# A causal attention stage whose row maxima are placed by batch instead of by group, and whose second score pass follows the first by eight units instead of twelve

## The chip, the core and the metric

The kernel runs on one core of a Trainium2 chip. The metric is the device time of one execution in microseconds, as the median of several runs. A profiled execution gives the trace: every instruction of the engines PE (matmul), PEld (its weight loads), DVE, ACT, POOL, and the DMAs, with start, length, line of the kernel, and what each waited for.

## The reference, cut to what matters

Two adaptive-layernorm transformer layers over 32 sequences of 256 tokens of 128 channels, all in float32. Layer 0 is plain attention and a feed-forward net with 4-bit rounding. Layer 1 is causal attention with 16 heads of 8 channels, then a mixture of experts of which 4 are active and each token takes 2. The change lies in layer 1's attention:

```python
qkv_heads = qkv.reshape(b, heads, s, -1)
q, k, v = jnp.split(qkv_heads, 3, axis=-1)
scale = 1.0 / np.sqrt(2.0 * hidden)
qk = jnp.einsum('bhse,bhte->bhst', q, k) * scale
mask = jnp.triu(jnp.full((s, s), -jnp.inf, dtype=jnp.float32), k=1)
attn = jax.nn.softmax(qk + mask, axis=-1)
out = jnp.einsum('bhst,bhte->bhse', attn, v).reshape(b, s, e)
```

A softmax needs each row's maximum. The kernel finds it in a first pass over the scores and subtracts it in a second.

## The kernel before, in words

The 8192 tokens are 16 groups (`NG`) of 512 (`TPG` = 4 tiles of 128); a group is two sequences, called batches here (`NB2` = 2, index j). The kernel has three stages, one after the other in time: layer 0, whose order is a written-out list of steps; the causal stage, with layer 1's attention and the choice of experts; and the expert stage, which works through tiles of tokens (`load`, `turn`, `tile_of`), and whose first loads need the memory of the causal stage.

The causal stage (from L655 on) is a loop over units, eight per group (`NU` = 8): four per batch, as j = n // 4. Its pieces:

- `maxima(u)` (L866, L873, L877): PE computes the scores c_s of a unit from qx and k and adds the mask; DVE reduces them in two instructions to negative maxima in c_mx.
- `gather_maxima`, `spread_maxima`, `place_maxima` (L887 to L907): once a group, DVE combines the eight units' maxima into c_m (four small instructions), PE transposes it into c_pm (PSUM), DVE copies it to c_mT, and SP writes it with 8 DMAs into a spare column of c_q. That column meets a column of ones in k, so that the second pass yields scores with the maximum already taken off.
- `probs(u)` (L920, L928, L931): PE computes these scores c_t from kx and q, ACT takes exp into c_p in two instructions, POOL zeroes what the mask forbids (two selects).
- `values(u, p)` (L948, L955): PE multiplies by v into c_po; after a batch's last unit DVE transposes c_po into c_o.
- For the next group: `c_start` (DVE statistics, then small POOL instructions), `c_norm` (ACT, xnc), `c_turn` (PE transposes c_xt, ACT makes c_hT), `c_qkv` (PE c_pq, DVE adds the bias into tok), `c_rows` (DVE transposes to q, k, v), `c_apart_q`, `c_apart_v` (ACT), `c_apart_k` (POOL, 1.6 us), `c_v` (PE transposes c_pv, ACT copies to c_vT).
- For groups behind: `c_ratio`, `c_gate` (DVE, and DMAs of the gate rows), `c_add` (POOL), then the d pieces: `d_start`, `d_norm`, `d_keep`, `d_turn` (PE d_xt, ACT d_hT), `d_logits` (PE d_pl, two ACT copies), and once per three groups `d_probs`, `d_share`, `d_rank`, `d_choose`, `d_pair`, `d_count`, `d_place`, and `d_scatter` (POOL indirect DMAs). `tables` (L1196 on, some 23 small DVE instructions) works out from the counts which rows the expert tiles load.

What sets the order is the list `beside` with `put(n, k, lead, piece)`: piece runs at every unit whose position in its group is n, for the group `lead` away; k = 0 is before the unit's `probs`, k = 1 after it. PE, DVE, ACT and POOL run this stage in exactly the written order; SP's DMAs keep close to it. In one step n the order is: `maxima` of unit n, `values` of the unit whose probs came two steps before (`BEHIND` = 2), pieces with k = 0, `probs` of unit n - `LAG`, pieces with k = 1. `LAG` is 12. So for 12 steps there are maxima alone, for 116 steps both, for 12 probs alone, and two more steps for values. What the last groups leave over (`remaining`) is fed into the first tiles of the expert stage.

All PE results of these pieces but c_s, c_t and c_po go through one PSUM buffer: pool `r_ps`, tag `ps`, one buffer. Whoever writes it waits until the one before has been read out. In the positions 1, 3, 5 and 7 of a group it is used by c_v, in 0, 2, 4 and 6 by c_qkv, each with k = 1; by c_turn at 0, spread_maxima at 1, d_turn at 2, d_count at 3, d_logits at 4 and 6, each with k = 0.

Of the kernel before, what the change touches and what calls it, by code (L numbers as in the profile page):

```python
# [10 lines left out]
F32 = mybir.dt.float32  # L11
# [8 lines left out]
P = 128  # L20
# [14 lines left out]
def adaln_two_layers(ctx: ExitStack, tc: tile.TileContext, ins, out: bass.AP):  # L35
    nc = tc.nc
    X = ins["L0_attn_X"].flatten_outer_dims()
    NTOK = X.shape[0]
    NG = NTOK // GT
# [87 lines left out]
    ident = const.tile([P, P], F32, tag="ident", name="ident")  # L127
# [6 lines left out]
    for l in range(2):  # L134
        sc = mp.tile([NB, D], F32, tag=f"sc{l}", name=f"sc{l}")
        nc.scalar.activation(sc, c_sb[l], AF.Silu)
        pt = mps.tile([P, 512], F32, tag="mps", name=f"mps_t{l}")
# [3 lines left out]
        pm = mps.tile([P, 512], F32, tag="mps", name=f"mps_m{l}")  # L141
# [8 lines left out]
        m = const.tile([D, 6, NB], F32, tag=f"mod{l}", name=f"mod{l}")  # L150
# [81 lines left out]
    with ExitStack() as ph:  # L232
# [10 lines left out]
        sb2 = ph.enter_context(tc.tile_pool(name="ab_sb2", bufs=2))  # L243
        sb3 = ph.enter_context(tc.tile_pool(name="ab_sb3", bufs=3))
        sb4 = ph.enter_context(tc.tile_pool(name="ab_sb4", bufs=4))
        ps = ph.enter_context(tc.tile_pool(name="ab_ps", bufs=3, space=PSUM))
# [408 lines left out]
    with ExitStack() as ph:  # L655
        one = ph.enter_context(tc.tile_pool(name="c_one", bufs=1))
        sb2 = ph.enter_context(tc.tile_pool(name="c_sb2", bufs=2))
# [3 lines left out]
        ps = r_ps  # L661
# [49 lines left out]
        NQ = NPOS // B  # L711
        NB2 = TPG // 2
        NU = NB2 * 2 * 2
        NBK = NB2 * 2 * NQ

        SEEN = [[(3, 0, 4 * B), (0, 4 * B, B)], [(2, 0, 3 * B), (1, 3 * B, 2 * B)]]
        SEES = [[(0, B, 4 * B), (3, 0, B)], [(1, 0, 3 * B), (2, 3 * B, 2 * B)]]
# [162 lines left out]
                    AX.X, ALU.max, negate=True,  # L880
                )

        def gather_maxima(g):
            mx = outs.pop(("mx", g)).rearrange("p (u s) l b -> p s u l b", s=2)
            m = sb2.tile([P, 4, NU // 2, NQ], F32, tag="m", name=f"c_m{g}")
            to = lambda b: m.rearrange("p l u b -> p b u l")[:, b, :, :]
            nc.vector.tensor_reduce(to(3), mx[:, 0, :, :, 0:4], AX.X, ALU.min)  # L887
            nc.vector.tensor_copy(to(0), mx[:, 0, :, :, 4])
            nc.vector.tensor_reduce(to(2), mx[:, 1, :, :, 0:3], AX.X, ALU.min)
            nc.vector.tensor_tensor(to(1), mx[:, 1, :, :, 3], mx[:, 1, :, :, 4], ALU.min)  # L890
            outs["m", g] = m

        def spread_maxima(g):

            m = outs.pop(("m", g))
            pt = outs["pm", g] = ps.tile([P, 512], F32, tag="ps", name=f"c_pm{g}")
            nc.tensor.transpose(pt[: 4 * NBK, :P], m.rearrange("p l u b -> p (l u b)"), ident)

        def place_maxima(g):
            pt = outs.pop(("pm", g))  # L900
            q = made[g]["q"].rearrange("p j (b n) -> p (j b) n", n=B)
            mT = sb2.tile([4 * NBK, P], F32, tag="mT", name=f"c_mT{g}")
            nc.vector.tensor_copy(mT, pt[: 4 * NBK, :P])
            for lane in range(4):
                for h in range(2):
                    row = lane * L + h * HR + C
                    nc.sync.dma_start(  # L907
                        q[row : row + 1, :, :], mT[lane * NBK : (lane + 1) * NBK, h * B : (h + 1) * B]
                    )

        def probs(u):
# [284 lines left out]
        def tables(kind):  # L1196
            nt, width = KINDS[kind]
            t = lambda n, shape, ty=F32: (one if kind else dw).tile([1] + shape, ty, tag=f"t_{n}{kind}", name=f"t_{n}{kind}")
            full, whole = t("full", [NP]), t("whole", [NP], I32)
            nc.vector.scalar_tensor_tensor(  # L1200
                full, nxt[0:1, :], float(width - 1) if kind == 2 else 0.0, region, ALU.add, ALU.subtract
            )
            nc.vector.tensor_copy(whole, full)
            nc.vector.tensor_scalar(whole, whole, width.bit_length() - 1, None, ALU.arith_shift_right)
            nc.vector.tensor_copy(full, whole)
            if kind > 0:
                nc.vector.scalar_tensor_tensor(full, done, float(-(ST // width)), full, ALU.mult, ALU.add)
            tri, begin = t("tri", [NP, NP]), t("begin", [NP])
            nc.vector.tensor_tensor(tri, earlier, full.unsqueeze(1).to_broadcast([1, NP, NP]), ALU.mult)
            nc.vector.tensor_reduce(begin, tri, AX.X, ALU.add)  # L1210

            off, last = t("off", [NP]), t("last", [NP])
            nc.vector.scalar_tensor_tensor(off, begin, float(-width), region, ALU.mult, ALU.add)
            if kind > 0:
                nc.vector.scalar_tensor_tensor(off, done, float(ST), off, ALU.mult, ALU.add)
            nc.vector.scalar_tensor_tensor(last, nxt[0:1, :], float(-width), region, ALU.add, ALU.max)
            nc.vector.tensor_tensor(coef[:, 0, :], off[:, 1:], off[:, : NP - 1], ALU.subtract)
            nc.vector.tensor_tensor(coef[:, 3, :], last[:, 1:], last[:, : NP - 1], ALU.subtract)
            past, part, to = t("past", [nt, NP - 1]), t("part", [nt, 4, NP - 1]), t("to", [nt, 4])
            nc.vector.tensor_tensor(  # L1220
                past, number[:, :nt].unsqueeze(2).to_broadcast([1, nt, NP - 1]),
                begin[:, 1:].unsqueeze(1).to_broadcast([1, nt, NP - 1]), ALU.is_ge,
            )
            nc.vector.tensor_tensor(
                part, past.unsqueeze(2).to_broadcast([1, nt, 4, NP - 1]),
                coef.unsqueeze(1).to_broadcast([1, nt, 4, NP - 1]), ALU.mult,
            )
            nc.vector.tensor_reduce(to, part, AX.X, ALU.add)
            nc.vector.tensor_scalar(to[:, :, 0], to[:, :, 0], off[:, 0:1], None, ALU.add)
            nc.vector.scalar_tensor_tensor(to[:, :, 0], number[:, :nt], float(width), to[:, :, 0], ALU.mult, ALU.add)  # L1230
            nc.vector.tensor_scalar(to[:, :, 3], to[:, :, 3], last[:, 0:1], None, ALU.add)
            nc.vector.tensor_tensor(to[:, :, 0], to[:, :, 0], to[:, :, 3], ALU.min)
            nc.vector.tensor_scalar(to[:, :, 2], to[:, :, 2], 1.0, None, ALU.add)
            told[kind] = t("told", [nt, 4], I32)
            nc.vector.tensor_copy(told[kind], to)
            if kind < 2:

                more = t("more", [NP])
                nc.vector.tensor_scalar(more, begin, -1.0, float(nt), ALU.mult, ALU.add)
                nc.vector.tensor_scalar(more, more, 0.0, None, ALU.max)  # L1240
                nc.vector.tensor_tensor(more, more, full, ALU.min)
                nc.vector.tensor_tensor(done, done, more, ALU.add)


        LAG = NU + 4
        BEHIND = 2
        beside = [[[], []] for _ in range(NU)]

        def put(n, k, lead, piece, *more):
            beside[n][k].append((lead, piece, more))  # L1250

        put(1, 0, -1, spread_maxima)
        put(1, 0, -1, place_maxima)
        put(0, 0, 1, c_turn)
        for i in range(TPG):
            put((2 + 2 * i) % NU, 1, 1 - (2 + 2 * i) // NU, c_qkv, i)
        for j in range(NB2):
            for n, k, piece, more in (
# [2 lines left out]
            ):  # L1261
                n += 4 * j
                put(n % NU, k, 1 - n // NU, piece, j, *more)
        put(0, 0, -1, gather_maxima)
        put(6, 0, -2, c_ratio)
        put(7, 0, -2, c_gate)
        put(7, 1, -2, c_add)
        for h in range(2):
            put(4 + 4 * h if h == 0 else 0, 0, 3 - h, c_start, h)
            put(1 + 2 * h, 1, 2, c_norm, h)  # L1270
            put(2 + h, 0, -3, d_start, h)
            put(5 + 2 * h, 1, -3, d_norm, h)
        put(4, 1, -3, d_keep)
        put(2, 0, -4, d_turn)
        put(4, 0, -4, d_logits, 0)
        put(6, 0, -4, d_logits, 1)
        last_of = lambda piece: lambda g, *more: piece(g, *more) if g == batch_of[g][-1] else False
        for n, k, lead, piece, *more in (
            (7, 1, -4, d_probs), (0, 1, -5, d_share), (3, 1, -5, d_rank), (4, 1, -5, d_choose), (5, 1, -5, d_pair, 0),
            (0, 1, -6, d_pair, 1), (1, 1, -6, d_pair, 2), (3, 0, -6, d_count), (4, 1, -6, d_place),  # L1280
        ):
            put(n, k, lead, last_of(piece), *more)
        for k in range(NT):
            put((5 + k) % NU, 1, -6 - (5 + k) // NU, last_of(d_scatter), k)
        put(4, 1, -8, lambda g: tables(0) if g == EARLY else False)
        for kind in (1, 2):
            put(3, 1, -6, lambda g, kind: tables(kind) if g == NG - 1 else False, kind)
        assert max(EARLY * NU + 8 * NU + 4, EARLY * NU + 6 * NU + 5 + NT - 1) < NG * NU + LAG + BEHIND

        def pieces(n, k):  # L1290
            for lead, piece, more in beside[n % NU][k]:
# [22 lines left out]

        def remaining():

            for n in range(len(units) + LAG + BEHIND, (NG + 8) * NU + 4):
                for k in range(2):
                    for lead, piece, more in beside[n % NU][k]:
                        g = n // NU + lead  # L1320
                        if 0 <= g < NG and piece(g, *more) is not False:
                            yield
# [185 lines left out]
```

## Time and profile before

| what | us |
|---|---|
| three runs | 1515.89, 1517.38, 1525.77 |
| median | 1517.38 |
| the profiled execution, its own time | 1526.12 |
| its span, first to last instruction | 1524.4 |
| causal stage in it: first c_s to last c_po | 415 to 962 |
| PE busy, 500 to 550 / 700 to 750 | 47.6 / 47.0 of 50 |
| DVE busy, the same | 41.6 / 42.8 of 50 |
| PE busy, 400 to 450 / 950 to 1000 | 35.0 / 32.4 of 50 |
| granted PE clock, the same | 0.80 / 0.73 |

The page gives busy time by engine, the span in 40 slices (digits are tenths; PEclk is the clock that the throttle granted), the chain that ended last, and groups of instructions. The timeline lists instructions in order of time, with the idle time of the engine before each and what ended it. The windows give busy time by engine for chosen stretches. Busy time of the whole span mixes three stages; the change touches the middle one.

### The profile page before, as it was taken

What the parts mean: (1) busy time and instruction counts of PE and PEld (TensorE: products, weight loads), DVE (VectorE), ACT (ScalarE), POOL (GpSimd) and SP (SyncE); (2) the same over time, 40 slices, a digit from 0 to 9 for tenths busy, and PEclk for the clock granted to TensorE, in tenths of its full rate; (3) what the DMA queues carried; (4) which work ended last, traced back from release to release, by engine and by line L of the source; (5) the groups of instructions that cost most, each with busy time, mean ns of one, the idle gap of its engine ahead of it and who ended that gap; (6) DMA issues with size and microseconds to landing.
All of it is one profiled execution on the core that took longest, in us unless ns stands there. A gap on an engine that the chain in (4) does not pass through costs nothing.

```text
span 1524.4 us, 33395 instructions
## 1 busy us (share of the span) xinstructions
PE 1382.3 (91%) x12505; PEld 1086.6 (71%) x12505; DVE 1001.1 (66%) x2219; ACT 777.8 (51%) x1551; POOL 744.8 (49%) x1079
## 2 busy tenths in 40 slices
PE   5888998987689999999999999598999999999997
PEld 4666665654357766667666667487999999999996
DVE  6799998989487888888988877146333333333332
ACT  5998877843255777767676667141222222222221
POOL 4767866664334665558668567426222222222122
PEclk9999999999799999999999999699999999999999
DMA  8000000000100000002102011856667777777760
GB/s 225 1 1 1 1 1 1 1 1 1 12 2 3 17 14 16 18 6 66 30 24 69 14 44 55 269 171 211 194 184 224 228 217 230 227 212 237 229 188 11
DMA packets 132065, 139.26 MB, mean 91 GB/s; under 512 B 14376, under 2 KB 105968, under 8 KB 131904
## 3 DMA queue, kind: packets, MB, share of 16 engines
q1 hardware_dynamic: 125600, 119.92, 26.9%
q0 software_dynamic: 6304, 17.21, 3.1%
q8 instruction: 99, 1.62, 0.4%
q14 instruction: 62, 0.51, 0.1%
HBM read 116.95 MB, written 19.61 MB: 90 GB/s over the span
## 4 chain that ended last, share of the span: by engine, by line
PE 69%; DVE 19%; ACT 4%; issue 3%; POOL 3%; SPq 1%; DMA 1%; POOLq 0%; DVEq 0%; ACTq 0%
PE d_y L1423 12%; PE d_pg L1437 11%; PE d_pu L1437 11%; PE c_s L866 6%; PE c_t L920 5%; PE c_po L948 4%; PE c_pq L803 3%; DVE c_mx L877 3%; PE c_s L873 2%; PE c_pv L851 2%; DVE qxh L382 2%; PE b_pu L485 2%; DVE sch L370 1%; DVE sch L378 1%; PE d_pl L1034 1%
## 5 line engine op out<-in xcount | busy, mean ns | idle before, releaser
L1443 DVE TENSOR_TENSOR d_h<-d_act,d_pu 128x512 f32<-128x512 f32 (+2 forms) x207 | 133.1, 644 | 298.9 <-PE d_pu L1437 274.9
L1441 ACT ACTIVATE d_act<-d_pg 128x512 f32<-128x512 f32 (+2 forms) x207 | 116.3, 562 | 394.8 <-PE d_pg L1437 348.2
L877 DVE TENSOR_REDUCE c_mx<-c_s 128x10 f32<-128x640 f32 x256 | 198.6, 817 | 55.0 <-PE c_s L873 54.9
L928 ACT ACTIVATE c_p<-c_t 128x640 f32<-128x640 f32 x256 | 166.2, 703 | 101.5 <-PE c_t L920 84.9
L1423 PE MATMUL d_y<-d_wd,d_h 128*128 128x128 f32 (+1 forms) x1656 | 209.6, 282 | 5.5 <-DVE d_h L1443 5.5
L1423 PEld LDWEIGHTS d_y<-d_wd,d_h 128*128 128x128 f32 (+1 forms) x1656 | 199.0, 192 | 20.8 <-DVE d_h L1443 6.8
L1437 PE MATMUL d_pg<-d_sT,d_wg 128*128 128x256 f32 (+1 forms) x924 | 204.3, 348 | 2.2 <-DMA d_wg<-in_L_ffn_w_dram 2.2
L1437 PE MATMUL d_pu<-d_sT,d_wu 128*128 128x256 f32 (+1 forms) x924 | 201.2, 345 | 0.0
L931 POOL TENSOR_SCALAR_AFFINE_SELECT c_p<-c_p 128x256 f32<-128x256 f32 x256 | 111.8, 445 | 140.1 <-ACT c_p L928 138.6
L1437 PEld LDWEIGHTS d_pu<-d_sT,d_wu 128*128 128x128 f32 x924 | 154.6, 192 | 16.5 <-DMA d_wu<-in_L_ffn_w_dram 0.7
L1437 PEld LDWEIGHTS d_pg<-d_sT,d_wg 128*128 128x128 f32 x924 | 142.1, 193 | 14.0 <-issue 2.6
L1462 POOL TENSOR_TENSOR d_o<-d_o,d_slot 128x256 f32<-128x256 f32 (+1 forms) x42 | 25.4, 605 | 248.7 <-DVE d_o L1461 239.0
L866 PEld LDWEIGHTS c_s<-c_k,c_qx 32*128 32x128 f32 x2048 | 99.8, 189 | 50.7 <-issue 21.9
L920 PE MATMUL c_t<-c_q,c_kx 32*128 32x256 f32 (+3 forms) x2048 | 131.1, 332 | 5.0 <-DVE c_mx L877 4.5
L1465 POOL DMA_INDIRECT out_dram<-d_o,d_slot x69 | 68.6, 994 | 136.4 <-DMA out_dram<-d_o,d_slot 125.1
L920 PEld LDWEIGHTS c_t<-c_q,c_kx 32*128 32x128 f32 x2048 | 102.8, 186 | 31.9 <-issue 9.6
L866 PE MATMUL c_s<-c_k,c_qx 32*128 32x256 f32 (+3 forms) x2048 | 123.2, 335 | 2.3 <-ACT c_p L928 1.5
L948 PE MATMUL c_po<-c_p,c_vT 128*32 128x256 f32 (+3 forms) x2048 | 100.1, 309 | 6.8 <-POOL c_p L931 6.4
L834 POOL TENSOR_SCALAR c_kx<-c_k,half 128x512 f32<-128x512 f32 x64 | 102.3, 1600 | 3.1 <-DVE c_k L819 3.0
L948 PEld LDWEIGHTS c_po<-c_p,c_vT 128*32 128x32 f32 x2048 | 55.4, 110 | 37.3 <-POOL c_p L931 8.3
L1150 POOL DMA_INDIRECT slots<-d_rows,d_index x64 | 64.8, 1013 | 17.1 <-issue 15.9
L485 PE MATMUL b_pu<-wupT,b_hqT 128*128 128x352 f32 x128 | 53.9, 505 | 20.5 <-DVE b_hh L491 20.5
(298 smaller groups left out, 2600.4 us busy)
## 6 DMA issues: line engine op xcount, KB each, us to landing
d_wg<-in_L_ffn_w_dram SPq DMA_DIRECT2D x84, 352.0 KB
d_wu<-in_L_ffn_w_dram SPq DMA_DIRECT2D x84, 352.0 KB
d_wd<-in_L_ffn_w_dram SPq DMA_DIRECT2D x84, 320.0 KB
d_slot<-slots SPq DMA_DIRECT2D x27, 387.0 KB
x<-in_L_attn_X_dram SPq DMA_DIRECT2D x16, 256.0 KB
d_rows<-gates SPq DMA_DIRECT2D x32, 128.0 KB
d_slot<-slots SPq DMA_DIRECT2D x15, 193.5 KB
d_wd<-in_L_ffn_w_dram SPq DMA_DIRECT2D x84, 32.0 KB
```

The source lines that it names most:

```text
L485: nc.tensor.matmul(pu[:, :HID0], lhsT=hT[:, i * P : (i + 1) * P], rhs=wT["up"], start=True, stop=True)
L834: nc.gpsimd.tensor_scalar(m["kx", j][:, :, h], m["k", j], half[:, h : h + 1], None, ALU.mult)
L866: nc.tensor.matmul(s[lane // 2][:, lane % 2, at : at + w], lhsT=qx[rows, NQ * e + b, :, :].rearrange("p h n -> p (h n)"), rhs=k[rows, e * ...
L877: nc.vector.tensor_reduce(mx[:, n, 2 * x : 2 * x + 2, :], s[x][:, :, 0:W].rearrange("p l (b n) -> p l b n", n=B), AX.X, ALU.max, negate=True,)
L920: nc.tensor.matmul(s[lane // 2][:, lane % 2, at : at + w], lhsT=kx[rows, (NQ * e + b) * P : (NQ * e + b + 1) * P], rhs=q[rows, (e + 1) * N ...
L928: nc.scalar.activation(t[:, :, 0:W], s[x][:, :, 0:W], AF.Exp, scale=SCALE1)
L931: nc.gpsimd.affine_select(out=diagonal, in_=diagonal, compare_op=ALU.is_ge, fill=0.0, base=1, pattern=[[0, 4], [2, B]] if sub else [[0, 2] ...
L948: nc.tensor.matmul(po[rows, (e + 1) * NPOS - w : (e + 1) * NPOS], lhsT=v[:, NQ * e + b, lane, :], rhs=p[lane // 2][:, lane % 2, at : at + ...
L1423: nc.tensor.matmul(y[k][:, b, :], lhsT=h[r0:r1, j, b * P : (b + 1) * P], rhs=wd[r0:r1, c, :], start=first and b == 0, stop=last and b == N ...
L1437: nc.tensor.matmul(to[:, j, :], lhsT=w[:, c * P : (c + 1) * P], rhs=hT, start=True, stop=True)
L1441: nc.scalar.activation(act[:, :m, :], pg[:, :m, :], AF.Silu)
L1443: nc.vector.tensor_tensor(h[:, :m, :], act[:, :m, :], pu[:, :m, :], ALU.mult)
```

## The change

The maxima are gathered, spread and placed per batch: `gather_maxima`, `spread_maxima` and `place_maxima` take j, work on the four units of that batch, and run at positions 4, 5, 5 for j = 0 and 0, 1, 1 of the next group for j = 1. The tiles m, c_pm and mT are half as wide, the DMAs carry 8 rows of 64 instead of 16; there are 8 for each batch. `LAG` is 8. Because c_o of a group is now complete four units earlier, the pieces behind it move four units ahead; d_turn and the first d_logits move by six.

```diff
-        def gather_maxima(g):
-            mx = outs.pop(("mx", g)).rearrange("p (u s) l b -> p s u l b", s=2)
-            m = sb2.tile([P, 4, NU // 2, NQ], F32, tag="m", name=f"c_m{g}")
+        def gather_maxima(g, j):
+            mx = outs["mx", g][:, 4 * j : 4 * j + 4].rearrange("p (u s) l b -> p s u l b", s=2)
+            m = sb2.tile([P, 4, 2, NQ], F32, tag="m", name=f"c_m{g}_{j}")
...
-            nc.tensor.transpose(pt[: 4 * NBK, :P], m.rearrange("p l u b -> p (l u b)"), ident)
+            nc.tensor.transpose(pt[: 4 * NBJ, :P], m.rearrange("p l u b -> p (l u b)"), ident)
...
-            q = made[g]["q"].rearrange("p j (b n) -> p (j b) n", n=B)
-            mT = sb2.tile([4 * NBK, P], F32, tag="mT", name=f"c_mT{g}")
+            q = made[g]["q"][:, j, :].rearrange("p (b n) -> p b n", n=B)
+            mT = sb2.tile([4 * NBJ, P], F32, tag="mT", name=f"c_mT{g}_{j}")
...
-        LAG = NU + 4
+        LAG = NU
...
-        put(1, 0, -1, spread_maxima)
-        put(1, 0, -1, place_maxima)
+        for j in range(NB2):
+            put((4 * j + 5) % NU, 0, -((4 * j + 5) // NU), spread_maxima, j)
+            put((4 * j + 5) % NU, 0, -((4 * j + 5) // NU), place_maxima, j)
...
-        put(0, 0, -1, gather_maxima)
-        put(6, 0, -2, c_ratio)
-        put(7, 0, -2, c_gate)
-        put(7, 1, -2, c_add)
+        for j in range(NB2):
+            put((4 * j + 4) % NU, 0, -((4 * j + 4) // NU), gather_maxima, j)
+        put(2, 0, -2, c_ratio)
+        put(3, 0, -2, c_gate)
+        put(3, 1, -2, c_add)
...
-            put(2 + h, 0, -3, d_start, h)
-            put(5 + 2 * h, 1, -3, d_norm, h)
-        put(4, 1, -3, d_keep)
-        put(2, 0, -4, d_turn)
-        put(4, 0, -4, d_logits, 0)
-        put(6, 0, -4, d_logits, 1)
+            put(6 + h, 0, -2, d_start, h)
+            put(1 + 2 * h, 1, -3, d_norm, h)
+        put(0, 1, -3, d_keep)
+        put(4, 0, -3, d_turn)
+        put(6, 0, -3, d_logits, 0)
+        put(2, 0, -4, d_logits, 1)
...
-            (7, 1, -4, d_probs), (0, 1, -5, d_share), (3, 1, -5, d_rank), (4, 1, -5, d_choose), (5, 1, -5, d_pair, 0),
-            (0, 1, -6, d_pair, 1), (1, 1, -6, d_pair, 2), (3, 0, -6, d_count), (4, 1, -6, d_place),
+            (3, 1, -4, d_probs), (4, 1, -4, d_share), (7, 1, -4, d_rank), (0, 1, -5, d_choose), (1, 1, -5, d_pair, 0),
+            (4, 1, -5, d_pair, 1), (5, 1, -5, d_pair, 2), (7, 0, -5, d_count), (0, 1, -6, d_place),
...
-            put((5 + k) % NU, 1, -6 - (5 + k) // NU, last_of(d_scatter), k)
-        put(4, 1, -8, lambda g: tables(0) if g == EARLY else False)
+            put((1 + k) % NU, 1, -6 - (1 + k) // NU, last_of(d_scatter), k)
+        put(0, 1, -8, lambda g: tables(0) if g == EARLY else False)
```

The later tables move by four as well, and `remaining` starts four units earlier. The rest of the kernel is unchanged.

## The prediction

> **What bounds the kernel now.** I read the page first, then the timeline of the causal stage unit by unit, then the waits of PE, then the windows of the stage's two ends.
>
> ```profile
> span 1524.4 us, 33395 instructions
> PE 1382.3 (91%) x12505; PEld 1086.6 (71%) x12505; DVE 1001.1 (66%) x2219; ACT 777.8 (51%) x1551; POOL 744.8 (49%) x1079
> PEclk9999999999799999999999999699999999999999
> ```
>
> The causal stage runs from about 415 to 962 us and PE is its bound: between 500 and 900 us it is busy 46 to 48 of every 50 us (windows), DVE 42. So a new wait of PE in the middle is paid in full, and a unit saved at an end is worth only what PE idles there.
>
> The measure I use is the step: in the timeline, from the start of one unit's first c_mx reduction to that of the next unit. The eight steps of a group are 4.37, 4.18, 3.60, 3.50, 3.67, 3.50, 3.72, 3.50 us (groups 2 and 3, 30.04 together). With the d pieces (groups 4 and 5) they are 4.37, 4.18, 4.38, 3.49, 4.13, 3.50, 4.13, 3.51 (31.70). Groups 4 to 14 take 366.4. The ends: unit 0 starts at 417.10; steps 0 to 8 take 22.9 and 8 to 12 take 11.9 (maxima alone), 12 to 16 take 18.5; group 15 from unit 120 to 127 takes 27.2; unit 127 starts at 924.03 and the last unit's first exp at 952.13, 28.1 later. Together 535.0 us.
>
> **The change part by part.** First, what a gather by batch adds. Step 1 holds the spread and the place; step 5 has the same work without them. Step 1, then step 5 (the columns are start, length, engine, line, operation):
>
> ```profile
> 535.54 0.30 PE L897 MATMUL c_pm<-ident,c_m 128*64 128x128 f32 x1
> 535.77 0.83 PE L920 MATMUL c_t<-c_q,c_kx 32*128 32x192 f32 x16
> 536.33 0.70 DVE L955 STREAM_TRANSPOSE c_o<-c_po 128x512 f32<-128x512 f32 x1
> 536.96 0.24 DVE L903 COPY c_mT<-c_pm 64x128 f32<-64x128 f32 x1
> 537.35 0.63 PE L851 MATMUL c_pv<-ident,c_vx 128*128 128x128 f32 x4 [0.75 <-DVE c_mT L903]
> ...
> 551.74 1.01 PE L920 MATMUL c_t<-c_q,c_kx 32*128 32x192 f32 x16
> 552.52 0.70 DVE L955 STREAM_TRANSPOSE c_o<-c_po 128x512 f32<-128x512 f32 x1
> 552.68 0.66 PE L851 MATMUL c_pv<-ident,c_vx 128*128 128x128 f32 x4
> ```
>
> c_pm, c_pv, c_pq and the turns share one PSUM buffer (tag ps, one buffer). In step 1 c_pv must wait until DVE has copied c_pm out, and DVE does that only behind the reduction and c_o. In step 5 c_pv follows c_t at once. The same wait, over 455 to 925 us:
>
> ```profile
> PE c_pv L851 <- DVE c_mT L903: 8.2, 11, 0.8
> ```
>
> The changed kernel spreads at steps 1 and 5. Step 5 then has the work of step 1: 4.18 - 3.50 = 0.69 (unrounded), once a group. From unit 13 on that is 15 times: +10.4. It is the surest term: step 1 is 4.18 or 4.19 and step 5 3.48 to 3.50 in nearly every group. Bounds 8 and 14. The four more gather instructions (0.45 us on DVE, step 4) fall in a step in which DVE idles for c_pq: nothing; without that cover 0.45 a group, 7.
>
> Second, the d pieces. Ratio, gate, add, start, keep, the second logits, the expert choice, scatters and tables all move by four units together, on every engine and queue alike. Projections, c_rows, c_apart and c_v repeat every four units, so the moved pieces meet the same neighbours (POOL's order past selects, c_kx and scatters included). Three things don't repeat: c_turn, c_norm, and d_turn with the first logits, which move by six. So d_norm stands behind c_norm on ACT in steps 1 and 3 and d_turn follows in step 4, where it had three steps of room. Step 3 now:
>
> ```profile
> 546.22 0.59 ACT L852 COPY c_vT<-c_pv 128x512 f32<-128x512 f32 x1
> 546.69 0.89 ACT L782 ACTIVATE xnc<-x,nmeanc,rstdc 128x128 f32<-128x128 f32 x2
> 547.60 0.72 PE L1034 MATMUL d_pl<-turner,d_hT 128*128 128x132 f32 x4
> ```
>
> Two xnd activations (0.45 each) will follow xnc at 547.58 and end at 548.47. d_turn takes the place of d_pl at 547.60; its fourth transpose would start at 547.93 and waits until then: 0.55, with the signal 0.6. Bounds 0.3 and 0.9. What is behind it, d_hT on ACT and c_pq, shifts with it. 13 turns fall in full steps: +7.8. In step 1 the extra xnd ends before d_pl needs ACT: nothing.
>
> Third, the wind-up. Units 8 to 11 are now full: 15.65 - 1.4 (units 8 and 9 have no values yet, 0.7 each) + 0.5 of the exp table's load of 1.28 = 14.75 against 11.9: +2.8. Gather and place at units 4 and 5, where DVE is the bound (5.00 of 5 us), cost +1.2 (before, step 9 to 10 was 3.59 against 2.3 without them). Units 12 to 16 now cost 15.07 against 18.5, because of the clock (granted clock is the third column from the end):
>
> ```profile
> 435.00:440.00 5.00, 4.09 (x49) 3.05 (x48) 5.00 (x9) 1.92 (x3) 0.00 (x0) 1.00 0.00 0
> 440.00:445.00 5.00, 2.26 (x25) 1.23 (x23) 4.76 (x16) 2.31 (x4) 2.15 (x5) 1.00 0.00 0
> 455.00:460.00 5.00, 5.00 (x40) 3.81 (x40) 3.07 (x4) 2.58 (x5) 0.87 (x3) 0.50 0.00 0
> ```
>
> After PE had 2.26 of 5 us the clock fell to half for some 11 us. The Trainium skill ("TensorE: Matmul & The Clock Gate", Part 1: The HAM clock gate) says an idle window of about 3.4 us brings the half clock; the longest gap here is 1.9 us, so the row is stricter than the rule. By the rule the new wind-up, whose longest gap (at unit 5) is again some 2 us, keeps its clock: 15.1. By the row a stretch at 45% is enough: 19.2. I take the first, since the two causes of the dip (c_xt's and c_mT's waits at units 8 and 9) no longer lie together without c_t between them; the other stays in the range. Wind-up: +2.8 + 1.2 - 3.4 = +0.6.
>
> Fourth, d pieces reach four units further into full steps: group 3 gets a turn (0.78) and a logits (0.46), +1.2; the fourth batch's d_probs falls in group 15 (that step took 5.45 in groups 9 and 12, +1.95 over 3.5), taken at +1.3; d_choose and d_pair now stand before c_mT, +1.0.
>
> Fifth, the wind-down. Four probs-only units less, at 28.1 for twelve, should save 8.2. But the tables of the first expert tiles (about 23 small DVE instructions) move from unit 132 to unit 128, ahead of the last c_mT:
>
> ```profile
> 930.40 0.24 DVE L903 COPY c_mT<-c_pm 64x128 f32<-64x128 f32 x1
> 930.71 5.74 SPq L907 DMA_DIRECT2D c_q<-c_mT  x8
> 935.13 0.14 DVE L1200 SCALAR_TENSOR_TENSOR t_full<-nxt,t_region 1x6 f32<-1x6 f32 x1
> 937.73 0.83 PE L920 MATMUL c_t<-c_q,c_kx 32*128 32x256 f32 x10 [0.25 <-DMA c_q<-c_mT]
> 939.19 0.15 DVE L1242 TENSOR_TENSOR t_done<-t_done,t_more 1x6 f32<-1x6 f32 x1
> ```
>
> From unit 127's start DVE has, in the built kernel's order: reduction 1.56, statistics 0.77, d_rank 2.16, gather 0.45, d_choose 1.18, tables 4.21, c_o 0.72, c_mT 0.24: 11.3. The DMAs, issued and landed, take 7.1 (930.64 to 937.73). So unit 132's c_t starts at 18.4; exp 0.8 later; three more units 6.0 (946.14 to 952.13): 25.2 against 28.1, so -2.9. Bounds: -8.2 if the DVE work fits elsewhere, +1 with the half clock. d_pl at unit 130 also waits for that c_mT. Behind the last exp nothing changes: POOL's selects, copies and scatters, then the loads.
>
> SP's place DMAs double from 128 to 256 at half the size. One costs 0.59 us to issue (median), so a group has 11.5 of 33 us with gate and rows 1.9 more. They hide: from c_mT's end to the c_t that needs it there are three steps, some 11.3 + 1.3 - 2.5 = 10.1 us, and the chain is 7.1. Queued between are gate (free since step 3) and rows (its buffer's scatter is two units old).
>
> **Sum**: 10.4 + 7.8 + 0.6 + 1.2 + 1.3 + 1.0 - 2.9 = +19.4; less some 2 that groups 7 to 14 hide in waits they have anyway (33.3 each against 31.7): **+17 us**. The traced execution took 1526.1 (span 1524.4), 0.6% over the median; I add the 17 to the median of 1517.4: **1534 us**.
>
> **The rivals.** (a) The middle has slack: the two new waits displace waits that stood there anyway. Takes off 18: about 1518, no change. It decides if step 5 stays at 3.5 and step 4 at 4.5. Against it: PE's steps 3, 5 and 7 have no wait to displace. For it: the turn's wait is under a microsecond and modelled from one step. (b) The clock falls again in the wind-up (+4.1) and, after PE's idle of about 4 us behind the tables, for the last units (+3): 1541. For it: 955 to 960 us, 0.63 after a gap of 5.6 us. (c) The placing DMAs come late: each us beyond the 10.1 costs 30 us over 30 batches; at one us 1564. Against it: PE's waits between 455 and 925 us name no DMA of c_q.
>
> **How the numbers follow.** Sum as worked out 0.58, its own range 1526 to 1543; (a) 0.20, 1509 to 1526; (b) 0.15; (c) 0.07. The range leaves out (c) and the lower part of (a): 1514 to 1548. About 1% (15 us) is what a measurement of this kernel tells from no change. Over +15: six tenths of the first case, most of (b), all of (c): 0.56. Faster by over 15: only a corner of (a) with the full 8 us at the end, 0.03. Same 0.41.
>
> **What would show it.** Steps 5 to 6 at 4.2 with c_pv waiting for c_mT in both halves of a group; step 4 at 5.0 with d_xt waiting for ACT xnd; no half clock between 440 and 465 us; about 23 table instructions before the last c_mT and c_t then waiting for a DMA; the stage some 17 us longer and everything behind it unchanged. Wrong: step 5 at 3.5, or c_t waiting for c_q in the middle.

## The result, and the profile after

The changed kernel takes 1539.6 us (median of 4 runs, 1539.0 to 1540.1) against 1518.0 for the kernel before beside it (1515.9 to 1525.8): a ratio of 1.0133, 95% interval 1.0097 to 1.0169. That is 21.6 us slower; 17 were forecast (1534, range 1514 to 1548).

The page of the changed kernel: its span, busy time by engine, and the granted clock in 40 slices.

```profile
span 1537.3 us, 33781 instructions
PE 1386.1 (90%) x12521; PEld 1084.7 (71%) x12521; DVE 1008.8 (66%) x2299; ACT 778.9 (51%) x1551; POOL 742.6 (48%) x1079
PEclk9999999999699999999999998699999999999999
```

PE's busy time grows by 3.8 us (1382.3 before), the span by 12.9: most of the loss is waiting, not work. In the clock's row the digits below 9 are slice 11, as before (where the stage begins), and now two slices near the stage's end (922 to 999 us) instead of one. A fall of 5 to 10 us elsewhere need not show in slices of 38 us; the windows are needed for it.

The medians differ by 21.6, more than the spans. The profiled execution of the kernel before was one of its long ones (1526.1), so a second trace was taken of it (e12). The steps, from one unit's first c_mx reduction to the next, summed by stretch:

| stretch | before | before again (e12) | changed | by the forecast |
|---|---|---|---|---|
| units 0 to 8 | 22.89 | 22.90 | 26.06 | +1.2 |
| 8 to 12 | 11.93 | 11.91 | 15.03 | +2.8 |
| 12 to 16 | 18.49 | 14.28 | 14.96 | -3.4, +0.7 wait |
| groups 2, 3 | 60.07 | 60.08 | 63.14 | +3.2 |
| groups 4 to 14 | 366.37 | 365.99 | 372.90 | +12.2 |
| group 15, to unit 127 | 27.16 | 27.26 | 31.48 | +2.6 |
| unit 127 to the last exp | 28.10 | 28.35 | 25.77 | -1.9 |
| together | 535.03 | 530.78 | 549.34 | +17.4 |

(The last column puts the forecast's terms where their instructions stand: the wait for c_mT at 0.69 and the turn at 0.6 a group, less the 2 us hidden.) So the stage grew by 14.3 us on the first trace and 18.6 on the second; from the last exp to the end it is 572.3 us in the first trace and 572.0 in the changed kernel, unchanged. The other 3 us of the medians are not located: two executions of one kernel and one of the other are traced.

**The second wait.** Step 5 of group 4 in the changed kernel, then the waits of PE from 455 to 925 us (us in total, times, longest):

```profile
558.32 0.24 DVE L903 COPY c_mT<-c_pm 32x128 f32<-32x128 f32 x1
558.71 0.63 PE L851 MATMUL c_pv<-ident,c_vx 128*128 128x128 f32 x4 [0.76 <-DVE c_mT L903]
```

```profile
PE c_pv L851 <- DVE c_mT L903: 18.2, 24, 0.8
```

Against 8.2 us in 11 waits before: 13 more at 0.77. Step 5 to 6 is 4.18 or 4.19 in every group from 1 to 14, where it was 3.48 to 3.50 in groups 2 to 14 of the first trace.

**The turn.** In step 4 the fourth transpose of d_xt waits for xnd, which now stands behind xnc on ACT (timeline of group 4):

```profile
551.92 0.88 ACT L782 ACTIVATE xnd<-x,nmeand,rstdd 128x128 f32<-128x128 f32 x2
552.47 0.14 PEld L199 LDWEIGHTS d_xt<-ident,xnd 128*128 128x128 f32 x1 [0.21 <-ACT xnd L782]
```

**The wind-up.** Unit 5's spread and what waits for it, then windows of the changed kernel (length; busy time of PE, PEld, DVE, ACT, POOL; granted clock third from the end):

```profile
431.94 0.29 PE L897 MATMUL c_pm<-ident,c_m 128*32 128x128 f32 x1 [0.96 <-DVE tok L806]
433.67 1.09 PE L851 MATMUL c_pv<-ident,c_vx 128*128 128x128 f32 x4 [1.45 <-DVE c_mT L903]
```

```profile
430.00:435.00 5.00, 2.59 (x25) 1.80 (x29) 4.48 (x14) 0.85 (x3) 0.00 (x0) 0.74 0.00 0
435.00:440.00 5.00, 5.00 (x46) 3.51 (x42) 3.21 (x5) 1.61 (x3) 0.00 (x0) 0.58 0.04 7
```

The half clock has not gone, as the forecast took it. There is none at units 12 to 14, but there is one at units 5 and 6: step 5 to 6 is 4.81, and c_pv takes 1.09 us where it takes 0.63 at full clock.

**The end.** The tables stand ahead of the last c_mT as foreseen. But the wait they bring is c_po's for c_o (c_po has one buffer, and DVE reaches c_o late), not d_pl's:

```profile
950.43 0.24 DVE L903 COPY c_mT<-c_pm 32x128 f32<-32x128 f32 x1
950.64 0.83 PE L948 MATMUL c_po<-c_p,c_vT 128*32 128x256 f32 x16 [4.14 <-DVE c_o L955]
```

### The profile page after: what moved, and what is told of

Its sections match the earlier page's. It is cut to its first block, busy times and chain, and to the rows that moved or that the text cites. A ratio compares the mean times of both kernels' runs of the same rounds, so it can differ in the third digit from the quotient of the medians.

```text
span 1537.3 us, 33781 instructions
## 1 busy us (share of the span) xinstructions
PE 1386.1 (90%) x12521; PEld 1084.7 (71%) x12521; DVE 1008.8 (66%) x2299; ACT 778.9 (51%) x1551; POOL 742.6 (48%) x1079
## 4 chain that ended last, share of the span: by engine, by line
PE 67%; DVE 17%; ACT 7%; issue 4%; POOL 3%; SPq 1%; DMA 1%; DVEq 0%; POOLq 0%; ACTq 0%
PE d_y L1425 12%; PE d_pg L1439 11%; PE d_pu L1439 11%; PE c_s L866 6%; PE c_t L920 4%; PE c_po L948 4%; PE c_pq L803 3%; DVE c_mx L877 3%; PE c_s L873 2%; PE c_pv L851 2%; DVE qxh L382 2%; PE b_pu L485 2%; PE d_pl L1034 1%; DVE sch L370 1%; PE b_py L527 1%
## 5 line engine op out<-in xcount | busy, mean ns | idle before, releaser
L948 PE MATMUL c_po<-c_p,c_vT 128*32 128x192 f32 (+3 forms) x2048 | 99.3, 309 | 12.3 <-POOL c_p L931 8.1
```

Source lines behind the costliest of these rows:

```text
L948: nc.tensor.matmul(po[rows, (e + 1) * NPOS - w : (e + 1) * NPOS], lhsT=v[:, NQ * e + b, lane, :], rhs=p[lane // 2][:, lane % 2, at : at + ...
```

## The experiments

The theory: two waits, c_pv's for c_mT in step 5 and d_xt's for xnd in step 4, and the tables ahead of the last placing, with the ends giving little back. Its rivals: the middle has slack and hides the waits; the clock's falls carry the loss; the placing DMAs come late. Of the last one there is no sign: from 455 to 925 us no wait of PE in the changed kernel names a DMA of c_q.

The ratio is to the kernel before on the same chip (e1 to e4 ran on one chip, e5 to e8 on a second, e9 to e12 on a third, where the kernel before takes 9 us longer).

| run | median us | before us | ratio, 95% interval |
|---|---|---|---|
| changed | 1539.6 | 1518.0 | 1.0133, 1.0097 to 1.0169 |
| e1 by batch, distance 12 | 1539.5 | 1519.2 | 1.0123, 1.0096 to 1.0149 |
| e2 d_norm first | 1535.4 | 1519.2 | 1.0107, 1.0081 to 1.0134 |
| e3 tables later | 1534.1 | 1519.2 | 1.0105, 1.0080 to 1.0129 |
| e4 c_pm in c_s | 1556.4 | 1519.2 | 1.0259, 1.0229 to 1.0289 |
| e5 c_pm in c_t | 1522.9 | 1519.3 | 1.0015, 0.9998 to 1.0032 |
| e6 before, c_pm in c_t | 1517.8 | 1519.3 | 0.9992, 0.9978 to 1.0005 |
| e7 e5 + e2 + e3 | 1513.9 | 1519.3 | 0.9966, 0.9950 to 0.9982 |
| e8 filled gap | 1537.8 | 1519.3 | 1.0114, 1.0089 to 1.0140 |
| e9 e1 without the wait | 1529.3 | 1528.4 | 1.0009, 0.9995 to 1.0023 |
| e10 e6, copy earlier | 1524.2 | 1528.4 | 0.9971, 0.9956 to 0.9986 |
| e11 e7 + e8, copy earlier | 1526.3 | 1528.4 | 0.9978, 0.9963 to 0.9993 |
| e12 before, traced again | 1528.8 | 1528.4 | one run |

Below, e2 to e8 are set against the changed kernel by their medians. The kernel before beside them took 1.2 to 1.3 us more than the one beside the changed kernel; by the ratios the gains of e2, e3, e5, e7 and e8 come out larger by that much.

### e1: half of the change alone

```diff
-        put(1, 0, -1, spread_maxima)   # and place; gather at (0, 0, -1)
+        for j in range(NB2):           # gather at 4j + 4
+            put((4 * j + 5) % NU, 0, -((4 * j + 5) // NU), spread_maxima, j)
...
         LAG = NU + 4
```

> Half of the change alone: the kernel before with its maxima gathered, spread and placed by batch (steps 4 and 5, 0 and 1), the second pass still twelve units behind, every d piece where it was. By the prediction's terms only the second PSUM wait (15 x 0.69 = 10.4 us) and the gather in units 4 and 5 (1.2) come: some +11 on the kernel before, about 1528, with steps 5 to 6 at 4.2 us and the waits of c_pv for c_mT at 25 x 0.8 instead of 11. If the waits displace others (slack), +3 or less. If the loss belongs to the shorter distance (turn, clock, ends), it stays within 5 us of the kernel before.

Measured +20, not +11: half of the change brings nearly the whole loss. The wait is as expected (step 5 to 6 at 4.18; 25 waits, 18.7 us). What was not expected are falls of the clock: in groups 8, 10, 11, 13 and 14, where the expert choice already holds PE up. Windows of e1, with step 5 of group 10 in them:

```profile
750.00:755.00 5.00, 3.65 (x56) 2.54 (x56) 4.71 (x11) 2.93 (x5) 1.72 (x4) 1.00 0.02 3
755.00:760.00 5.00, 5.00 (x60) 3.59 (x58) 4.27 (x8) 2.01 (x6) 2.14 (x3) 0.66 0.02 2
```

The stretch of the kernel before that answers to it (748 to 758 us) keeps clock 1.00, with PE at 4.22 of 5 us in its first half. The falls of groups 10 and 13 lie in steps 5 and 6, at the new wait; those of groups 8, 11 and 14 lie in steps 3 and 4, where the first trace of the kernel before has one too (group 8). That the wait brings more of them is seen over the runs: the mean granted clock of e1's six is 0.964 against 0.969 for the kernel before on that chip, while that of e9, which lacks the wait, is 0.965 against 0.967 on its own. Summed against e12: units 0 to 16 +3.2 (half clock at unit 5), groups 2 to 14 +14.6 (13 x 0.69 = 9.0; the other 5.6 are steps at the lower clock, as 4.96 and 4.86 in group 10), group 15 +0.7, the end +2.0 (clock 0.83 and 0.82 at 950 to 960): 20.4.

The other half, the shorter distance, thus nets about nothing. From e1's trace to the changed kernel's, units 8 to 16 take 3.8 more, groups 2 and 3 1.7 and group 15 3.6, while groups 4 to 14 take 6.3 less (they have fewer falls of the clock) and the end 4.6 less.

### e2 and e3: the turn and the tables

```diff
+            put(1 + 2 * h, 1, -3, d_norm, h)
             put(1 + 2 * h, 1, 2, c_norm, h)
             put(6 + h, 0, -2, d_start, h)
-            put(1 + 2 * h, 1, -3, d_norm, h)
```

> The changed kernel with d_norm ahead of c_norm in ACT's order of steps 1 and 3, so that xnd is ready when d_xt comes and only c_xt, four steps later, sees the later xnc. If step 4's wait for xnd is what the turn costs: 13 x 0.37 = 5 us less than the changed kernel by its trace (7.8 by the prediction), step 4 to 5 back from 4.82 to 4.45, about 1534. If the wait only displaces another (PE waits for DVE there next), less than 2 us and step 4 stays near 4.8.

Measured 4.2 us less than the changed kernel. The intervals of the two ratios overlap, so the trace has to carry it; the same holds for e3 and e8. In e2's group 4 xnd is done (551.16) before d_xt begins:

```profile
550.27 0.89 ACT L782 ACTIVATE xnd<-x,nmeand,rstdd 128x128 f32<-128x128 f32 x2
551.06 0.87 ACT L782 ACTIVATE xnc<-x,nmeanc,rstdc 128x128 f32<-128x128 f32 x2
551.19 0.66 PE L199 MATMUL d_xt<-ident,xnd 128*128 128x128 f32 x4
```

Step 4 to 5 is 4.36 instead of 4.83. Over groups 3 to 14 the differences of this step add up to 4.3 us: nothing in groups 9 and 14, where the expert choice holds PE up anyway.

```diff
-        put(0, 1, -8, lambda g: tables(0) if g == EARLY else False)
+        put(4, 1, -8, lambda g: tables(0) if g == EARLY else False)
```

> The changed kernel with the tables of the first expert tiles four units later (unit 132, as far behind the last placing as before the change). If they hold up the last c_mT and c_o: the 5.3 us of DVE work in front of them go, the way from unit 127 to the last exp falls from 25.8 to about 20.5, and the kernel gains 4 to 5 us (1534). If c_o at unit 131 or another wait takes over, 1 us or nothing; if the tables now run late for the expert loads, the gain in the stage comes back behind it and the time stays at 1539.

Measured 5.5 us less. c_mT is copied 6.7 us after unit 127's start instead of 10.9, c_po waits for nothing there, and the way to the last exp is 21.3 us instead of 25.8. (Group 15 takes 1.3 more in this trace, with the clock at 0.50 from 930 to 935 us, so the stage is 3.3 shorter in it.) The end of e3, to be held against the two lines above:

```profile
947.06 0.24 DVE L903 COPY c_mT<-c_pm 32x128 f32<-32x128 f32 x1
947.28 0.75 PE L948 MATMUL c_po<-c_p,c_vT 128*32 128x256 f32 x16
```

### e4 and e5: c_pm out of the shared buffer

```diff
-            pt = outs["pm", g] = ps.tile([P, 512], F32, tag="ps", name=f"c_pm{g}_{j}")
+            pt = outs["pm", g] = outs["cs"][1][:, 1, 512 - P : 512]   # e4: second c_s tile
...
+            pt = outs["pm", g] = outs["ct"][1][:, 1, 512 - P : 512]   # e5: second c_t tile, behind c_t
```

> The changed kernel with c_pm in the unused last 128 columns of the same unit's second c_s tile instead of the shared PSUM buffer, so c_pv no longer waits for c_mT (except at the very last placing). By the prediction's term steps 1 and 5 lose 0.69 each, 30 times: -20 us, about 1519, steps 1 to 2 and 5 to 6 at 3.5; the clock dip behind unit 5 of group 0 may go too (-3). If the middle is bound elsewhere (DVE's reduction, c_mx of the next unit waiting for a c_s tile that is now held until c_mT is out), steps stay above 4 and the gain is 5 us or less.

It is 17 us slower than the changed kernel: steps 1 to 2 and 5 to 6 are 4.63. The wait moved and grew. Waits of PE in e4, 455 to 925 us (L901 is c_pm there):

```profile
PE c_s L901 <- DVE c_mx L877: 24.5, 27, 1.4
```

The free columns lie in the bank that DVE is reducing, so c_pm waits for the reduction, and everything behind it on PE with it. The Trainium skill ("PSUM — Partial Sum Buffer", PSUM bank collisions raise a hardware error) asks for waits by bank and not by address; the built kernel waits that way, 0.9 us on average.

> The changed kernel with c_pm written into the unused last 128 columns of the same unit's second c_t tile, behind c_t, where nothing has read yet; c_mT is copied out of it behind DVE's next transpose (1 us later). c_pv then waits for no copy. By the prediction's term: 29 x 0.69 = -20 us against the changed kernel, about 1519, steps 1 to 2 and 5 to 6 at 3.5 us. If DVE's reduction is the bound right behind PE, steps go no lower than about 3.9 and the gain is 8; if the later copy makes the placing late, c_t waits for a DMA of c_q and the time stays at 1539 or above.

Measured 16.7 us less than the changed kernel, of the 20 expected; in its trace the stage is 19.7 shorter. Both waits of a group are gone, that of the kernel before and the new one. (The first placing of group 0 stays in the shared buffer, here and in e6 to e11.) No wait of PE for c_mT is left, and steps 1 to 2 and 5 to 6 are 3.49 to 3.50 in most groups. In groups 7, 10 and 13 they stay at 4.2, with step 2 to 3 and 6 to 7 shorter for it (3.7, 3.6). The later copy made no DMA late: c_t waits 1.4 us in all for c_q's DMAs.

### e6, e9 and e10: the same wait in the kernel before, and in e1

```diff
-            nc.tensor.transpose(pt[: 4 * NBK, :P], m.rearrange("p l u b -> p (l u b)"), ident)
+            def pull():   # run by probs, behind c_t
+                pt = outs["pm", g] = outs["ct"][1][:, 1, 512 - P : 512]
+                nc.tensor.transpose(pt[: 4 * NBK, :P], m.rearrange("p l u b -> p (l u b)"), ident)
+                place_maxima(g)   # e9, e10, e11; in e5, e6, e7 at k = 1
```

> The kernel before, placing by group and twelve units behind, with c_pm in the c_t tile in the same way. The wait stands there once a group: 14 x 0.69 = -10 us, about 1508, step 1 to 2 at 3.5. If the term is a wait that only displaces others, 2 us or less.

Missed: 1.6 us less, with no change inside the interval. Groups 2 to 14 are 8.6 us shorter than in the first trace, as the term says (e5 takes 18.2 off the same groups of the changed kernel, where there are two such waits); the end is 6.0 longer. SP's queue in e6:

```profile
920.26 0.37 SPq L1014 DMA_DIRECT2D d_rows<-gates  x1
920.72 5.64 SPq L913 DMA_DIRECT2D c_q<-c_mT  x8
```

c_mT was ready at 917.53. In the built order a load of d_rows slipped ahead of the last placing on SP, waited for its own buffer, and held the placing back by 3.2 us; c_t of unit 132 then waits 2.7 us for it.

> As e6 (the kernel before with c_pm in the c_t tile), but with the copy called right behind c_pm, which puts the last placing DMAs ahead of d_rows in SP's order again. In e6 that order held the last c_q back by 3.2 us and c_t of unit 132 by 2.7. If it is what hid the gain of the middle (8.6 us), the time falls by 3 to 6 us against e6, to about 1513; if not, it stays at 1518.

With the queue's order restored: 4.2 us below the kernel before, 2.6 more than e6 gained, just short of the 3 to 6 expected. The end is back to 29.3 us from e6's 34.1. There is a new wait. The copy now comes ahead of exp in the order, both read the same c_t tile, and ACT waits for DVE (e10, 455 to 905 us):

```profile
ACT c_p L940 <- DVE c_mT L912: 10.7, 11, 1.0
```

c_vT behind it on ACT is late, d_xt waits 0.31 us for c_vT to free the shared buffer, and step 2 to 3 is 4.75 instead of 4.38 in most groups with d pieces.

> Placing by batch at distance twelve, as in e1, with c_pm in the c_t tile from group 1 on, and the copy called right behind it. Against e1 it lacks the wait of c_pv and nothing else. If the +20 of e1 are this wait and the clock falls that it brings: within 4 us of the kernel before without the wait (e10), about 1516. If four more gather instructions, two copies and twice as many placing DMAs cost by themselves, it stays 8 us or more above e10.

1.0 us above the kernel before, where e1 was 20 above. The 19 between them are not the new wait alone: e9 lacks the kernel before's wait as well, so its fair partner is e10. Against e10 it is 5.1 longer; in the traces 3.9 of that are units 0 to 8, where the clock falls at unit 5 (26.78 against 22.89), since group 0 still places through the shared buffer. That leaves about 15 of e1's 20 to the new wait with the falls of the clock, which agrees with the 14.6 in groups 2 to 14 of its trace. In those groups e9 takes 0.7 us more than e10: the four more gather instructions, the second copy and twice as many DMAs cost next to nothing there. (e9 isn't free of waits either: ACT waits for c_mT 19 times, 17.1 us, as in e10.)

### e8 and e12: the clock

```diff
+            if g == 0 and j == 0:
+                idle = ps_o.tile([P, 512], F32, tag="po", name="idle")
+                for n in range(8):
+                    nc.tensor.transpose(idle[:, n % 4 * P : (n % 4 + 1) * P], ident, ident)
```

> The changed kernel with eight more transposes of ident (0.17 us each at full clock) by PE between c_pm and c_pv of unit 5 of group 0, into the c_po buffer that nothing uses yet: work in the gap of 1.5 us behind which PE's granted clock fell. If the clock follows PE's idle time there, 430 to 440 us stay at 1.00, step 5 to 6 falls from 4.81 to about 3.3, and the wind-up (units 0 to 16) takes 2 to 3 us less; if it follows the whole stretch before (2.6 of 5 us busy) or something else, the clock falls all the same and the time is that of the changed kernel or 0.5 us more.

The clock stays whole there, and step 5 to 6 of group 0 is 3.57 instead of 4.81. The same windows in e8:

```profile
430.00:435.00 5.00, 4.40 (x51) 3.35 (x51) 4.11 (x7) 1.81 (x3) 0.00 (x0) 1.00 0.02 5
435.00:440.00 5.00, 4.05 (x49) 3.00 (x47) 5.00 (x8) 1.76 (x4) 0.00 (x0) 1.00 0.01 2
```

Units 0 to 8 take 24.5 instead of 26.1. The whole kernel takes 1.8 us less, which the intervals do not tell from nothing, and in the trace the stage is no shorter (549.0), since group 15 takes 32.7 instead of 31.5. The fall at unit 5 itself is no chance: all eight traces that place by batch without the filling have it (step 5 to 6 from 4.70 to 5.68), and the two with it, e8 and e11, do not (3.57). So 1.04 us of PE work there prevents it. What in PE's idle time brings it is less clear: by the clock's record it falls at 432.35, only 0.13 us into the gap of 1.45.

> The kernel before once more, for a second trace of it. Its first profiled execution took 1526.1, some 7 us over the middle of its runs (1519), and held the half clock at 455 to 465, 675 to 680 and 955 to 960 us. If such falls of the clock are what moves it from run to run, an execution near 1518 lacks one or more of them and has the same steps elsewhere (4.37, 4.18, 3.60, 3.50...); if they are in every run, the 7 us lie outside the causal stage.

This execution (one run, on another chip) has the same plain groups to within 0.02 us. It differs where the clock does: units 12 to 16 take 14.28 and not 18.49, group 8 takes 34.36 and not 35.88. (Groups 9 and 12 are 0.4 to 0.6 longer.) Windows of e12, in the same place as those the forecast read:

```profile
440.00:445.00 5.00, 2.25 (x25) 1.41 (x26) 4.76 (x15) 2.27 (x4) 2.37 (x5) 1.00 0.00 0
455.00:460.00 5.00, 4.72 (x74) 3.48 (x71) 3.68 (x6) 2.86 (x5) 2.33 (x4) 1.00 0.00 0
```

PE was as idle here (2.25 of 5 us) as in the first trace (2.26), and the clock did not fall. It did not fall in e1 either, which has the same gap of 1.71 us there. In the first trace it fell only at 454.5, with two windows in between in which PE was mostly busy:

```profile
445.00:450.00 5.00, 4.00 (x49) 2.94 (x50) 4.12 (x6) 2.58 (x5) 2.73 (x2) 1.00 0.03 5
450.00:455.00 5.00, 4.53 (x42) 2.81 (x40) 4.01 (x9) 3.57 (x6) 0.15 (x1) 0.95 0.02 5
```

So it is not shown that this dip brought the fall. The order alone does not bring the fall: it stands in one of the three traces, and 4.2 us of the first trace are such a fall. The three were not all taken on one chip, but the clock also varies on one: over the 51 runs of the kernel before on e12's chip (1522 to 1538 us) its mean is 0.970 in the ten shortest and 0.963 in the ten longest. The stretch behind the last exp is 579 us on this chip against 572, which is why the total is no lower.

### e7 and e11: a faster version (e5, e2 and e3 together; with the filling of e8)

> The changed kernel with all three: c_pm in the c_t tile, d_norm ahead of c_norm, the tables at unit 132. If the three terms add up: -20 - 4.5 - 4.5 = -29 against the changed kernel, 1510, some 8 below the kernel before; if they share one slack, no lower than the best of the three alone, 1519.

The three terms nearly add up: 25.7 us below the changed kernel against 29 expected, and 5.4 below the kernel before (ratio 0.9966). Its trace is of an execution 6 us above its median (1519.9), with falls of the clock behind the expert choice in groups 7, 9, 12 and 14 (0.66 to 0.93 in windows of 5 us).

> The three changes of e7 with the eight filling transposes of e8 at unit 5 of group 0 (and that unit's copy ahead of DVE's transpose of q). If they add up: e7's 1514 less 2 to 4 us (step 5 to 6 of group 0 was 5.68, at full clock some 3.6), 1511, which is below both the kernel before and the changed one. If the clock falls elsewhere instead, 1514.

The wind-up is 2.2 us shorter (units 0 to 8: 24.63 against 26.84), but the earlier copy puts the wait of ACT into steps 2 and 6 as in e10 (2 to 3: 4.84 against 4.13). Against the kernel before on its chip it gains less than e7 on its own: 2.1 us. e7 has the lowest ratio of the twelve, though that of e10 (0.9971) is not told from it; e7 with the filling and the later copy was not tried.

## Why the prediction was right, and where by luck

The time and the sign were right, and the likeliest case was the one that held. That the sum came so near is in part luck: the single terms were less good than their sum, and their errors cancelled.

- **Second wait (+10.4): right in size and place, with one effect left out.** Each step lengthens by 0.69 as read from step 1. In groups 2 to 14 taking both waits out of the changed kernel gives 18.2 us (e5), taking the one out of the kernel before gives 8.6 (e6): the second is worth 9.6, against 13 x 0.69 = 9.0. What the term left out is that a longer wait can come with falls of the clock: at the old distance (e1) it costs about 15. And one wait was counted twice: the 15.07 of units 12 to 16 (3.67 + 4.18 + 3.72 + 3.50) holds the wait of unit 13 already, so the sum was 0.7 too high.
- **Turn (+7.8): right in kind, too large.** In a plain group step 4 to 5 is 0.47 above that of e2, not 0.6, and not all 13 pay it: 4.3 (e2).
- **What the middle hides (2): 5.75.** A plain group with d pieces went from 31.70 to 32.85, +1.15; eleven of them make 12.65. Groups 4 to 14 grew by 6.9. The rest is the expert choice: it took 17.3 us on top of plain groups before (e12: 365.99 - 11 x 31.70) and 11.55 after (372.90 - 11 x 32.85). The likely reason is that its DVE work now stands beside waits that PE has anyway; e2, which gains nothing in groups 9 and 14, agrees, but no run takes the expert choice out. So the first rival's mechanism was there, with a third of the size that it needed. (The forecast's 33.3 us is the mean of groups 4 to 14; groups 7 to 14 have 33.9 in the first trace, so there was more to hide in than it saw.)
- **Wind-up (+0.6): wrong.** The failed step is the choice of the rule over the row: that the new order, with its two causes apart, keeps its clock. The clock fell at unit 5, so units 0 to 8 took +3.2 and not +1.2. The rule and the row were also both read too firmly. The 1.9 us called the longest gap is an idle time of PEld; PE's own was 1.71, and the fall came 9.5 us after its end. Of the warm-up, the Trainium skill ("TensorE: Matmul & The Clock Gate", Part 1: The HAM clock gate) also says that the window is free-running and that the same kernel differs from run to run; e12 beside the first trace shows that a fall can differ too. The -3.4 of units 12 to 16 was the gain over one unlucky execution: against e12 there is none, and the wind-up costs 7.0 (0.7 of it the second wait).
- **Group 15 (+1.3 for d_probs): too small.** The stretch takes 4.2 more instead of 2.6: the step of d_probs is 5.44 as foreseen, but the clock falls behind it (0.73 and 0.59 at 925 to 935 us), and step 5 to 6 takes 5.10.
- **Wind-down (-2.9, +1.0): right in size.** -2.6 against e12 for the two together, and the cause of so small a gain, the tables, is confirmed by e3. The last c_t that needs a placing starts 18.7 us after unit 127, against 18.4 worked out. The wait named was the wrong one: PE stands at c_po for c_o, ahead of where d_pl would wait.
- **Placing DMAs: hidden, as worked out.** No wait of PE for c_q's DMAs stands in the changed kernel from 455 to 925 us, though there are twice as many of them and one takes 0.63 us to issue (median), not 0.59.

The first rival's time should have read 1516, 18 under 1534. The clock's rival (b), at 1541, is nearer to the truth in its mechanism than the chance of 0.15 says: the clock did fall in the wind-up and in the last units (0.50 for 3.4 us behind the wait of 4.14). The forecast's sum met the result because groups 4 to 14 grew by 5.3 less than reckoned, while the wind-up and group 15 took 7.3 more.

## What to carry to other kernels

Ahead of splitting a handover into halves, count the buffers that each half passes through: here a single PSUM buffer turned one wait a group into two, and moving the small tile into free columns of a tile that nobody has read yet took both waits out and gave 16.7 us back, about half of it for the wait that the kernel before has too. When taking such a wait away, look for who else uses the new place (a reduction in its bank, an exp behind the copy, a DMA queue whose order shifts): in e4, e6 and e10 each removal brought a new one. And trace the kernel before twice when a term rests on a fall of the clock in it.

## What the runs showed of the hardware

PE's clock fell to half without a long idle time of PE. At unit 5 of the changed kernel it fell 0.13 us into a gap of 1.45 us, and the longest gap before that, since the clock's rise at 422.1, was 0.96. In the first trace it fell 9.5 us after a gap of 1.71, and in two other traces the same gap brought no fall. Eight transposes, 1.04 us of PE in the gap at unit 5, kept the clock whole in both traces that had them. In the traces' clock records every half-clock stretch inside the stage lasts 3.41, 6.83 or 10.24 us. And a wait of 0.69 us a group that looks local came with more than its own length: in e1 the 13 of groups 2 to 14 are 9.0 us, and these groups took 14.6 more.
